# Reciprocal roots of the layer norms: a ScalarE seed with one Newton step in place of a bit guess with three

## The chip, the cores and the metric

The kernel runs on one core of a Trainium2 chip. The metric is the device time of one launch in microseconds; for a version with several runs it is their median. A core has five engines that work side by side, each through its own queue in order: TensorE (PE; its weight loads are listed apart as PEld), VectorE (DVE), ScalarE (ACT), GpSimd (POOL) and SyncE (SP). Engines wait for each other through semaphores. Transfers between memory and the core go through 16 DMA engines.

## The reference

The input is 32 images of 128 channels by 56 by 56. What is computed, cut to what matters:

```python
x = x + conv3x3(sign(groupnorm(x)), sign(w)) * Alpha      # layer 0
t = to_tokens(x)                                          # 32 x 3136 x 128
t = t + attention(_ln_t(t))       # q * sum(k * v), no softmax
t = t + top_2_of_8_experts(_ln_t(t))
x = from_tokens(t)

def _ln_t(v, eps=1e-5):
    m = jnp.mean(v, axis=-1, keepdims=True)
    s = jnp.var(v, axis=-1, keepdims=True)
    return (v - m) / jnp.sqrt(s + eps)
```

So each token needs two reciprocal roots of (variance + eps), one for each layer norm: the first scales the attention's inputs, the second the router's logits and the experts' inputs.

## The kernel before

**Tiling.** One image after another is worked on, in steps that overlap with those of the images before and after. Its 3136 tokens are 25 chunks of 128 (the last has 64), so that a number for each token of an image is a tile of 128 x 25 in float32. Chunks go in blocks of four (seven blocks), and the convolution in seven strips of eight rows.

**The stages of one image.** Group-norm sums on ScalarE (L579), a matmul for the group means (L592), signs on ScalarE (L599), the convolution (L642) and its addition on VectorE (L653), transposes to tokens (L667) with ScalarE's copies out of PSUM (L673), and the first statistics (L682). Then come the variance (`var_of`, L500 to L505) and the reciprocal root (`rstd_of`, L511 to L527). With it ScalarE scales the tokens (L735), TensorE makes their Gram matrix (L744), and a chain of small steps that alternate between TensorE and VectorE makes the attention's factor (L754 to L808). Projections (L863), their eviction with the root as the scale (L877), additions and the second statistics (L890, L893) follow, then the second variance and root. The router uses it: logits (L951 to L955), two largest experts (L938 to L962), their ratio as an exponential on ScalarE (L973), gates (L977 to L1012).

**Experts.** The first 8 to 12 chunks of an image go densely through all experts: gate rows are spread from memory (tile `bc`), VectorE multiplies (L1141), TensorE accumulates (L1159, in pool `ff`), VectorE adds (L1170). The other chunks of the first 28 images are sorted by pair of experts. GpSimd scatters their rows (L1365), and after each group of images (8, 8, 8 and 4) tiles of 128 rows are loaded, turned (L1669, L1675), multiplied by the two experts' weights (L1687), scaled by ScalarE (L1705, L1712), added (L1717, L1722), stored, gathered by GpSimd (L1444), turned back (L1459) and copied out (L1467).

**The order.** `plan_image` and `plan_group` enter each step with a due time, an engine, an assumed duration and the steps that it comes after (`at`). `in_order` is a list scheduler that takes these numbers and writes one order for all engines. A step whose work is given as a list of durations is split into links, with a lag of 0.12 us assumed between them, and the planner may put other work between two links. The order of each engine's queue is that order; the chip then runs each queue strictly in it. What the planner assumes therefore decides the order, not the time.

**The lines of the change.** `rstd1` and `rstd2` (steps due at s + 44 and s + 119, where s is the image's base time) call `rstd_of`. It has eleven VectorE instructions on 128 x 25: a shift of the variance's bits (L511), a subtraction from a constant (L518), which together give a first guess, and three Newton steps of three instructions each (L523, L525, L527), each needing the result of the one before. 32 images with two norms make 64 such roots. The three constants are filled at the start (L247 to L255). The convolution weights come through seven transfers issued from ScalarE's queue (L323 to L326), summed on VectorE (L350), and made into signs on ScalarE (L356). PSUM has a pool `ps` of five buffers, shared by most steps.

Of the kernel before, what the change touches and what calls it, by code (L numbers as in the profile page):

```python
# [46 lines left out]
I32 = mybir.dt.int32  # L47
U32 = mybir.dt.uint32
AF = mybir.ActivationFunctionType
ALU = mybir.AluOpType  # L50
# [4 lines left out]
C = 128  # L55
# [21 lines left out]
    mybir.EngineType.SP,  # L77
}
ON_POOL = 8
NEWTON = 3  # L80
IN_FLIGHT = 4
HELD, LOADS, LOAD_LANDS = 3, 4, 10.0

# [102 lines left out]
def conv_attn_moe_kernel(  # L186
# [19 lines left out]
    nc = tc.nc  # L206
    n_img, _, height, width = x.shape
    n_tok = height * width
    n_conv = height // ROWS
    n_ck = -(-n_tok // C)  # L210
# [24 lines left out]
    const = ctx.enter_context(tc.tile_pool(name="const", bufs=1))  # L235
# [11 lines left out]
    nc.vector.memset(ones, 1.0)  # L247
    ones_h = const.tile([C, C], BF16, name="ones_h")
    nc.vector.memset(ones_h, 1.0)
    one_i = const.tile([C, 1], I32, name="one_i")  # L250
    nc.vector.memset(one_i, 1)
    guess = const.tile([C, 1], I32, name="guess")
    nc.vector.memset(guess, 0x5F3759DF)
    m_one = const.tile([C, 2], F32, name="m_one")
    nc.vector.memset(m_one, -1.0)  # L255

# [61 lines left out]
    for j in range((K_REP + 1) // 2):  # L318
        flat = tok_all[j].rearrange("p c e -> p (c e)")
        z_sb += [flat[:, : TAPS * C], flat[:, TAPS * C : 2 * TAPS * C]]  # L320
    for k in range(2):
        load_x(0, nc.sync, k, 2)
    nc.scalar.dma_start(rv_bc, rv.to_broadcast([C, K_REP]))  # L323
# [144 lines left out]
    def at(due, key, engine, work, do, *args, after=(), take=(), free=(), delay=0.0, slack=0.0):  # L468


        if isinstance(work, float):
            steps[key] = Step(due, key, engine, work, do, args, after, take, free, delay, slack, 0.0)
            return
        running = []

        def go_on():
            if not running:
                running.append(do(*args))
            next(running[0], None)

        lag = LAG if isinstance(work, list) else 0.0
        for j, w in enumerate(work):
            last = j == len(work) - 1
            part = key if last else (*key, "part", j)
            steps[part] = Step(
                due, part, engine, w, go_on, (), [(*key, "part", j - 1)] if j else after,
                [] if j else take, free if last else [], delay if last else 0.0, slack, lag,
            )
# [6 lines left out]
    def var_of(stats, var, name):  # L495
# [8 lines left out]
        yield  # L504
        nc.vector.scalar_tensor_tensor(var, var, 1.0 / C, diff, ALU.mult, ALU.add)  # L505

    def rstd_of(var, dst, name):

        square = spool.tile([C, n_ck], F32, tag=f"square{name}", bufs=1, name="square")
        shape = [C, n_ck]  # L510
        nc.vector.tensor_tensor(  # L511
            square.bitcast(I32),
            var.bitcast(I32),
            one_i.to_broadcast(shape),
            ALU.logical_shift_right,
        )
        yield
        nc.vector.tensor_tensor(  # L518
            dst.bitcast(I32), guess.to_broadcast(shape), square.bitcast(I32), ALU.subtract
        )  # L520
        for _ in range(NEWTON):
            yield
            nc.vector.tensor_mul(square, dst, dst)  # L523
            yield
            nc.vector.scalar_tensor_tensor(square, square, -0.5, var, ALU.mult, ALU.mult)  # L525
            yield
            nc.vector.scalar_tensor_tensor(dst, square, 1.5, dst, ALU.add, ALU.mult)  # L527

    def sent_from(i, g):

# [13 lines left out]
    def plan_image(i: int):  # L544
        s = base(i)
        d = {"x": x_all[i % HELD], "tok": tok_all[i % HELD]}
# [59 lines left out]
        for k in range(n_load):  # L606
# [3 lines left out]
                after=[("load", i, k - 1) if k else ("load", i - 1, 1)]  # L610
# [4 lines left out]
        for j in range(GN_PARTS):  # L615
# [6 lines left out]
                after=[("gn_neg", i), ("conv", i - 1, min(j + 1, n_conv - 1))],  # L622
# [3 lines left out]
            after=[("gn_sum", i, j) for j in range(GN_PARTS)],  # L626
# [4 lines left out]
            after=[("gn_mean", i), ("gn_sign", i - 2, GN_PARTS - 1)], free=[("ps", ("gn_mean", i))],  # L631
# [53 lines left out]
        def var1():  # L685
            d["var1"] = spool.tile([C, n_ck], F32, tag="var1", name=f"var1_{i}")
            d["r1"] = spool.tile([C, n_ck], F32, tag="r1", name=f"r1_{i}")
            yield from var_of(st1, d["var1"], "1")

        def rstd1():  # L690
            yield from rstd_of(d["var1"], d["r1"], "1")

        for b in range(n_conv):
            at(
                s + 5.5 * b, ("conv", i, b), "PE", 1.75, conv, b,
                after=[("gn_sign", i, j) for j in range(min(b + 2, GN_PARTS))]
# [5 lines left out]
                after=[("conv", i, b)], free=[("ps", ("conv", i, b))],  # L702
            )
        for g in range(n_blk):
# [5 lines left out]
                after=[("conv_add", i, b), ("xt", i, g - 1)] + sent_from(i - HELD, g),  # L710
# [4 lines left out]
                after=[("xt", i, g)], free=[("ps", ("xt", i, g))],  # L715
# [3 lines left out]
                after=[("xt_out", i, g), ("var1", i - 2)],  # L719
# [3 lines left out]
            after=[("stats1", i, g) for g in range(n_blk)]  # L723
            + [("project_out", i - 2, 8), ("rstd1", i - 1)],
        )
        at(s + 44, ("rstd1", i), "DVE", [0.10] * (2 + 3 * NEWTON), rstd1, after=[("var1", i)])


        def scaled(g):
# [87 lines left out]
        for g in range(n_blk):  # L817
# [3 lines left out]
                after=[("rstd1", i), ("scaled", i, g - 1), ("scaled", i - 1, last_b)], take=["y"],  # L821
# [3 lines left out]
                after=[("scaled", i, g), ("gram", i, g - 1), ("kv_7", i - 1)],  # L825
# [90 lines left out]
        def var2():  # L916
            d["var2"] = spool.tile([C, n_ck], F32, tag="var2", name=f"var2_{i}")
            d["r2"] = spool.tile([C, n_ck], F32, tag="r2", name=f"r2_{i}")
            yield from var_of(st2, d["var2"], "2")

        def rstd2():
            yield from rstd_of(d["var2"], d["r2"], "2")

# [147 lines left out]
            after=[("project_add", i, j) for j in range(last_q + 1)]  # L1071
            + [("rstd2", i - 1), ("dense_gates", i - 2), ("row_scalars", i - 2)],
        )
        at(s + 119, ("rstd2", i), "DVE", [0.10] * (2 + 3 * NEWTON), rstd2, after=[("var2", i)])
        at(s + 125, ("route_1", i), "DVE", [0.28] * 3, route_1, after=[("rstd2", i)] + routed)
        at(s + 126, ("route_2", i), "DVE", [0.28] * 6, route_2, after=[("route_1", i)])
        at(s + 128, ("route_3", i), "DVE", [0.28] * 4 + [0.38], route_3, after=[("route_2", i)])
# [800 lines left out]
```

## Time and profile before

| | |
|---|---|
| median of 3 runs | 2172.5 us (2171.1 to 2178.69) |
| the profiled execution, in all | 2270.18 us |
| its span, first to last instruction | 2268.4 us |
| mean granted TensorE clock | 0.975 of full speed |
| ScalarE activation table loads | 1, 1283 ns (L579) |
| the five lines of `rstd_of`, VectorE busy | 11.5 + 11.4 + 34.7 + 35.1 + 34.6 us |

The profiled execution takes longer than the runs without a profile, so a saving that is read from it is carried over as a share. In the profile's tables, each group of instructions has one row: line, engine, operation, what it writes and reads, shape, count, then busy time in us, mean ns of one, and the idle time of the engine just before them with what ended it. A row of waits reads: engine and line that waited, what it waited for, us in total, times, the longest. A row of a stage reads: from and to in us, length, then busy us and count of each engine, TensorE's granted clock, the DMA engines' mean busy share and GB/s. Busy time on VectorE counts overlapping records once.

### The profile page before, as it was taken

The page shows a single profiled execution, that of the slowest core. Times are in us where ns is not written, and L with a number is a line of the kernel's source. Part 1 is how long each engine was busy: PE and PEld are TensorE (multiplying, and loading weights), DVE is VectorE, ACT ScalarE, POOL GpSimd, SP SyncE. Part 2 cuts the span into 40 slices and gives each one's busy share as a digit, 9 for nine tenths or more (in the row PEclk, how much of TensorE's full clock was granted, in tenths as well). Part 3 has the DMA queues.
Part 4 walks back from the last instruction along what each step waited for, and adds up shares of the span by engine and source line. Part 5 has one row for each costly group of instructions (what it writes and reads, how often), then busy time and mean ns, then how long its engine had stood idle before and what let it go on. Part 6 is the DMA issues. An engine that isn't in the chain of part 4 may idle for free.

```text
span 2268.4 us, 45320 instructions
## 1 busy us (share of the span) xinstructions
PE 2103.4 (93%) x12074; PEld 1449.1 (64%) x12074; DVE 1970.1 (87%) x6074; ACT 1531.2 (68%) x4917; POOL 1041.1 (46%) x1013
## 2 busy tenths in 40 slices
PE   5899999899999999789999999988999999999888
PEld 2666656557777776457676776655676666676544
DVE  4899999999989999688888889988898798789865
ACT  5667776668888887468777867655877776574311
POOL 3044443333433325466443644676654446233563
PEclk9989999999999999899999999999999999999999
DMA  4155544465665565377667766667767777878788
GB/s 166 30 175 177 167 153 141 138 184 184 203 186 165 176 181 168 110 219 252 194 202 220 226 198 202 215 214 240 225 195 232 217 203 247 249 214 270 222 278 273
DMA packets 324364, 448.58 MB, mean 198 GB/s; under 512 B 61832, under 2 KB 222128, under 8 KB 324112
## 3 DMA queue, kind: packets, MB, share of 16 engines
q1 hardware_dynamic: 294384, 382.80, 54.7%
q0 software_dynamic: 28144, 56.14, 8.2%
q10 hardware_dynamic: 1584, 6.75, 0.8%
q8 instruction: 102, 1.67, 0.3%
q14 instruction: 150, 1.23, 0.2%
HBM read 319.51 MB, written 126.00 MB: 196 GB/s over the span
## 4 chain that ended last, share of the span: by engine, by line
PE 42%; DVE 5%; DMA 3%; issue 2%; ACT 2%; another core or an unknown queue 1%; SPq 0%; POOL 0%; DVEq 0%; ACTq 0%; POOLq 0%
PE ff L1159 14%; PE to L1687 7%; PE cv L642 6%; PE q L863 3%; PE gram L744 3%; PE turn L1669 2%; PE back_ps L1459 2%; PE xt L667 2%; DVE gated L1141 1%; DMA back<-res,res_no 1%; PE l L1114 1%; DMA out_dram<-o 1%; PE ff L1153 1%; DMA bc<-gp 0%
## 5 line engine op out<-in xcount | busy, mean ns | idle before, releaser
L1365 POOL DMA_INDIRECT rows<-tok,row_no x428 | 524.3, 1225 | 570.5 <-ACT tok L1358 235.8
L1159 PE MATMUL ff<-gated,ew_d 128*128 128x512 f32 (+1 forms) x1536 | 711.5, 592 | 23.8 <-DVE gated L1141 19.8
L1444 POOL DMA_INDIRECT back<-res,res_no x428 | 485.4, 1134 | 464.1 <-PE back_ps L1459 264.1
L1141 DVE TENSOR_TENSOR gated<-tt,bc 128x1024 f32<-128x1024 f32 x384 | 450.7, 1180 | 92.2 <-PE ff L1159 29.9
L642 PE MATMUL cv<-xs,w_bin 128*128 128x440 bf16 (+3 forms) x2016 | 429.8, 362 | 18.5 <-ACT xs L599 10.0
L1159 PEld LDWEIGHTS ff<-gated,ew_d 128*128 128x128 f32 x1536 | 274.5, 193 | 258.6 <-issue 202.2
L1705 ACT ACTIVATE v<-to,t_in 128x128 f32<-128x128 f32 x528 | 255.3, 484 | 138.1 <-PE to L1687 74.6
L642 PEld LDWEIGHTS <-w_bin 128*128 128x128 bf16 x2016 | 200.1, 100 | 187.8 <-issue 38.3
L1687 PEld LDWEIGHTS to<-ew_s,turned 128*128 128x128 f32 x2112 | 260.8, 194 | 57.8 <-issue 32.4
L877 ACT ACTIVATE qs<-q,r 128x136 f32<-128x136 f32 (+1 forms) x800 | 247.6, 406 | 70.3 <-PE q L863 35.1
L1687 PE MATMUL to<-ew_s,turned 128*128 x2112 | 273.3, 279 | 18.2 <-ACT turned L1675 8.1
L735 ACT ACTIVATE y<-tok,r 128x128 f32<-128x128 f32 (+1 forms) x800 | 257.0, 428 | 24.3 <-PE gram L744 10.4
L863 PE MATMUL q<-move,x 128*128 128x144 f32 (+1 forms) x1600 | 239.9, 295 | 12.7 <-issue 3.7
L863 PEld LDWEIGHTS q<-move,x 128*128 128x128 f32 (+1 forms) x1600 | 213.6, 193 | 42.4 <-issue 21.1
L744 PEld LDWEIGHTS gram<-y 128*128 128x128 f32 (+1 forms) x1600 | 203.3, 192 | 53.9 <-issue 40.4
L744 PE MATMUL gram<-y 128*128 128x129 f32 (+1 forms) x1600 | 217.8, 281 | 12.9 <-issue 8.1
L682 DVE BATCH_NORM_STATS2 st<-tok 128x6 f32<-128x128 f32 (+1 forms) x800 | 185.4, 279 | 31.9 <-ACT tok L673 26.9
L1712 ACT ACTIVATE w<-to,t_in 128x128 f32<-128x128 f32 x528 | 208.6, 395 | 0.0
L893 DVE BATCH_NORM_STATS2 st<-tok 128x6 f32<-128x128 f32 (+1 forms) x800 | 198.1, 284 | 6.3
L673 ACT COPY tok<-xt 128x512 f32<-128x512 f32 (+1 forms) x224 | 121.2, 561 | 99.9 <-PE xt L667 71.6
L653 DVE SCALAR_TENSOR_TENSOR x<-cv,alpha_col,x 128x448 f32<-128x448 f32 x224 | 151.3, 676 | 40.1 <-PE cv L642 7.2
L890 DVE TENSOR_TENSOR tok<-tok,qs 128x408 f32<-128x408 f32 (+1 forms) x288 | 156.1, 542 | 29.4 <-ACT tok L882 24.1
(229 smaller groups left out, 2896.0 us busy)
## 6 DMA issues: line engine op xcount, KB each, us to landing
bc<-gp SPq DMA_DIRECT2D x368, 512.0 KB
x<-in_x_dram SPq DMA_DIRECT2D x116, 392.0 KB
t_in<-rows SPq DMA_DIRECT2D x528, 66.0 KB
res<-v SPq DMA_DIRECT2D x132, 256.0 KB
out_dram<-o SPq DMA_DIRECT2D x100, 256.0 KB
out_dram<-tt SPq DMA_DIRECT2D x92, 256.0 KB
rows<-zeros SPq DMA_DIRECT2D x116, 66.0 KB
rows<-tok,row_no POOLq DMA_INDIRECT x428
```

What stands on the lines that cost most here:

```text
L642: nc.tensor.matmul(cv[:, r0:r1, c0:c1], lhsT=w_bin[:, t, :], rhs=xs[:, b * ROWS + dy + r0 : b * ROWS + dy + r1, dx + c0 : dx + c1], start= ...
L735: nc.scalar.mul(y[:n, j, :C], d["tok"][:n, c, :C], d["r1"][:n, c : c + 1])
L744: nc.tensor.matmul(d["gram"], lhsT=y[:n, j, :C], rhs=y[:n, j, :], start=(c == 0), stop=(c == n_ck - 1),)
L863: nc.tensor.matmul(p[:n, k, :], lhsT=d["x"][:, c * C : c * C + n], rhs=move, start=True, stop=True,)
L877: nc.scalar.mul(qs[:n, k, :], p[:n, k, : C + N_EXP], d["r1"][:n, c : c + 1])
L1141: nc.vector.tensor_tensor(g[:, :, :n], d["tt", b][:, :n].unsqueeze(1).to_broadcast([C, 2, n]), d.pop(("bc", b, k))[:, :, :n], ALU.mult,)
L1159: nc.tensor.matmul(d["ff", b][:, :n], lhsT=ew_d[:, e * C : (e + 1) * C], rhs=g[:, j, :n], start=False, stop=(e == N_EXP - 1),)
L1365: dma = nc.gpsimd.indirect_dma_start(out=groups[group]["rows"], out_offset=bass.IndirectOffsetOnAxis(ap=d["row_no"][:n, c - n_dense : c - ...
L1444: dma = nc.gpsimd.indirect_dma_start(out=d["back", c][:n, :], out_offset=None, in_=groups[group]["res"][: quads_of(group) * WIDE, :], in_o ...
L1687: nc.tensor.matmul(p[:, k, j, :], lhsT=t[:, n * C : (n + 1) * C], rhs=ew_s[:, bass.ds(d["cols", q][j][n], C)], start=True, stop=True,)
L1705: nc.scalar.activation(d["v", q][:, n, :], p[:, k, 0, :], AF.Identity, bias=row[:, C + 2 : C + 3], scale=row[:, C : C + 1],)
L1712: nc.scalar.mul(d["w", q][:, n, :], p[:, k, 1, :], row[:, C + 1 : C + 2])
```

## The change

The two instructions of the bit guess and two of the three Newton steps go. A new helper, `seed_of`, has ScalarE write the logarithm of the variance and then, in place, the exponential of minus half of it. Two new steps, `seed1` and `seed2`, each with an assumed 0.45 us of ScalarE, stand between variance and root; the root has three VectorE links left. The two integer constants go, and at the start of the kernel the activation table set that has both functions is loaded ahead of the first transfers.

```diff
-NEWTON = 3
...
-    one_i = const.tile([C, 1], I32, name="one_i")
-    nc.vector.memset(one_i, 1)
-    guess = const.tile([C, 1], I32, name="guess")
-    nc.vector.memset(guess, 0x5F3759DF)
...
+    nc.scalar.preload_act_table_set("natural_log_exp_and_others")
     for k in range(2):
         load_x(0, nc.sync, k, 2)
     nc.scalar.dma_start(rv_bc, rv.to_broadcast([C, K_REP]))
...
+    def seed_of(var, dst):
+        nc.scalar.activation(dst, var, AF.Ln)
+        nc.scalar.activation(dst, dst, AF.Exp, scale=-0.5)
+
     def rstd_of(var, dst, name):
 
         square = spool.tile([C, n_ck], F32, tag=f"square{name}", bufs=1, name="square")
-        shape = [C, n_ck]
-        nc.vector.tensor_tensor(
-            square.bitcast(I32),
-            var.bitcast(I32),
-            one_i.to_broadcast(shape),
-            ALU.logical_shift_right,
-        )
+        nc.vector.tensor_mul(square, dst, dst)
         yield
-        nc.vector.tensor_tensor(
-            dst.bitcast(I32), guess.to_broadcast(shape), square.bitcast(I32), ALU.subtract
-        )
-        for _ in range(NEWTON):
-            yield
-            nc.vector.tensor_mul(square, dst, dst)
-            yield
-            nc.vector.scalar_tensor_tensor(square, square, -0.5, var, ALU.mult, ALU.mult)
-            yield
-            nc.vector.scalar_tensor_tensor(dst, square, 1.5, dst, ALU.add, ALU.mult)
+        nc.vector.scalar_tensor_tensor(square, square, -0.5, var, ALU.mult, ALU.mult)
+        yield
+        nc.vector.scalar_tensor_tensor(dst, square, 1.5, dst, ALU.add, ALU.mult)
...
+        def seed1():
+            seed_of(d["var1"], d["r1"])
+
...
-        at(s + 44, ("rstd1", i), "DVE", [0.10] * (2 + 3 * NEWTON), rstd1, after=[("var1", i)])
+        at(s + 43, ("seed1", i), "ACT", 0.45, seed1, after=[("var1", i)])
+        at(s + 44, ("rstd1", i), "DVE", [0.10] * 3, rstd1, after=[("seed1", i)])
...
+        def seed2():
+            seed_of(d["var2"], d["r2"])
...
-        at(s + 119, ("rstd2", i), "DVE", [0.10] * (2 + 3 * NEWTON), rstd2, after=[("var2", i)])
+        at(s + 118, ("seed2", i), "ACT", 0.45, seed2, after=[("var2", i)])
+        at(s + 119, ("rstd2", i), "DVE", [0.10] * 3, rstd2, after=[("seed2", i)])
```

## The prediction

> **What bounds the kernel now.** I read the page's first two parts, then the table of busy time by stage, because an average over a kernel whose mixture of work changes says little.
>
> ```profile
> PE 2103.4 (93%) x12074; PEld 1449.1 (64%) x12074; DVE 1970.1 (87%) x6074; ACT 1531.2 (68%) x4917; POOL 1041.1 (46%) x1013
> ```
>
> TensorE is busy for 93% of the span, VectorE for 87%. Only 165 us of the span have no matmul, and that is all that any change away from TensorE can win. By stage (length, then busy us of each engine):
>
> ```profile
> core 0: us, PE busy (x) PEld busy (x) DVE busy (x) ACT busy (x) POOL busy (x), PEclk, DMA share, GB/s
> 120.00:540.00 420.00, 392.64 (x2204) 257.30 (x2203) 407.87 (x1428) 289.34 (x969) 179.95 (x164) 0.98 0.50 161
> 540.00:900.00 360.00, 353.04 (x2277) 260.40 (x2277) 337.96 (x1065) 304.50 (x995) 136.62 (x110) 1.00 0.60 181
> 900.00:1500.00 600.00, 561.73 (x3296) 392.91 (x3295) 525.36 (x1644) 433.60 (x1398) 319.70 (x272) 0.97 0.68 209
> 1500.00:1920.00 420.00, 386.19 (x2296) 275.81 (x2295) 349.98 (x1057) 292.60 (x925) 236.35 (x206) 0.97 0.73 217
> 1920.00:2100.00 180.00, 179.88 (x978) 122.51 (x977) 155.41 (x368) 103.16 (x319) 58.98 (x52) 1.00 0.81 244
> 2100.00:2268.40 168.40, 143.17 (x520) 78.41 (x519) 113.21 (x214) 32.23 (x92) 85.71 (x74) 0.93 0.79 258
> ```
>
> From 120 to 540 us VectorE sets the pace: 12.1 us idle of 420, while TensorE idles 27.4. From 540 to 900 TensorE does (7.0 idle of 360). From 900 to 1920 neither is full (TensorE idle 72.1, VectorE 144.7 of 1020), so chains between engines end the waits there. From 1920 to 2100 TensorE never stops; after that the tail waits for transfers. The first 120 us, with 33.2 us of TensorE idle, are the start.
>
> The lines that the change touches, and two waits:
>
> ```profile
> L525 DVE SCALAR_TENSOR_TENSOR square<-square,var 128x25 f32<-128x25 f32 x192 | 35.1, 183 | 3.3
> L523 DVE TENSOR_TENSOR square<-r 128x25 f32<-128x25 f32 x192 | 34.7, 181 | 2.9 <-DVE r L527 0.2
> L511 DVE TENSOR_TENSOR square<-var,one_i 128x25 int32<-128x25 int32 x64 | 11.5, 180 | 0.7
> L973 ACT ACTIVATE ratio<-ratio 128x25 f32<-128x25 f32 x32 | 7.8, 243 | 46.1 <-DVE ratio L970 27.1 <-DVE best L944 5.6 <-DVE res_no L1439 5.3
> ```
>
> ```profile
> PE ff L1159 <- DVE gated L1141: 19.8, 20, 2.6
> ACT ratio L973 <- DVE ratio L970: 27.1, 14, 4.3
> ```
>
> The second line of the pair is the nearest relative of what is added: an exponential of a 128x25 tile on ScalarE, between two VectorE steps.
>
> The timeline of VectorE at one root (start, duration) shows how much the links really occupy:
>
> ```profile
> 377.77 0.17 DVE L511 TENSOR_TENSOR square<-var,one_i 128x25 int32<-128x25 int32 x1
> 377.86 0.29 DVE L893 BATCH_NORM_STATS2 st<-tok 128x6 f32<-128x128 f32 x1
> 378.06 0.17 DVE L518 TENSOR_TENSOR r<-guess,square 128x25 int32<-128x25 int32 x1
> 378.14 1.22 DVE L1141 TENSOR_TENSOR gated<-tt,bc 128x1024 f32<-128x1024 f32 x1
> 379.28 0.18 DVE L523 TENSOR_TENSOR square<-r 128x25 f32<-128x25 f32 x1
> 379.37 0.58 DVE L890 TENSOR_TENSOR tok<-tok,qs 128x408 f32<-128x408 f32 x1
> ```
>
> A link is recorded as 0.17 us, but other work starts 0.09 us after it. Where nothing can be put between (at 336.9 us of the same timeline) links follow each other every 0.22 us. From start to next start, the links between 60 and 540 us take 0.144 us on average; later about 0.15 to 0.19.
>
> [...] The trace of before shows one load, 1.283 us (L579, at 8.15 us); no switch is in it. The changed kernel's instruction order holds one load too, the preload, so I count no switch. [...] the trace has a median of 226 and a mean of 243 for L973, and I use 0.23.
>
> **Part by part.** The sum is made against the profiled execution: span 2268.4, 2270.2 in all. That is 4.5% above the median of 2172.5, so I carry a share, not microseconds, over.
>
> Removed: 64 roots (32 images, two each), with 8 of 11 links gone: shift, subtraction and two Newton steps. 512 x 0.144 = 74 us of VectorE issue time; by recorded durations 512 x 0.18 = 92. Per root 8 x 0.144 = 1.15 us. Two constant fills at the start (0.06 us each) go as well: nothing waits for them, zero.
>
> Added on ScalarE: 128 activations x 0.243 = 31 us. Its idle time is 737 us, so as volume that is covered, least well from 540 to 900, where it is busy 304.5 of 360. The two are dependent, so one seed takes about 0.46 us.
>
> Added waits: logarithm for variance, Newton step for seed. The exponential of L973 starts 0.03 to 0.04 us after its input is written when ScalarE is free, and VectorE follows a ScalarE result in 0.03 at best; the free round trip is 0.04 + 0.46 + 0.03 = 0.53 us. In the changed order, VectorE has other work between variance and Newton step in 62 of 64 roots, most often two to five instructions, some 1.7 us by this trace's durations; in the VectorE-bound stage the second root's cover is mostly one 128x512 addition, 0.6 us. So a free ScalarE costs VectorE nearly nothing. A late one (L973 started up to 2.4 us late between 540 and 900) costs up to 2 us, behind which all of VectorE's queue stands, the gating products for TensorE first. Bounds per root: 0 and 2 us; I take 0.1. On the other side, the logarithm at the head of ScalarE's queue holds back what is queued behind it, evictions of matmul results above all, as L973 does: 46.1 us idle in 32 times, 1.44 each. TensorE has five PSUM buffers in hand against that. In the waits, TensorE stands for ScalarE 36.5 us between 120 and 1920; I let that grow by a tenth, 4 us (bounds 0 and 32, half a us for each root).
>
> What is late next, by stage. From 120 to 540, 16 roots free 16 x 1.15 = 18.4 us of a full VectorE; TensorE's floor, at the 1.9% idle that it reaches in the next stage, is 392.6 / 0.981 = 400, or 20 less. TensorE's waits put down to VectorE there are 10.7 us, to ScalarE 11.4, part of them VectorE's delay passed on. I take 12. From 540 to 900 TensorE is full: of 3.7 us of waits for VectorE I take 1.5. From 900 to 1500 the waits for VectorE are 12.5 us, but VectorE had 75 us of idle time and was late for other reasons: a third, 4. From 1500 to 1920, 10.8 us: a quarter, 3. After 1920: 0.5. From 60 to 120 one image runs nearly alone and the chain itself counts: eight links of 0.2 less a round trip of 0.53 is 1.1 us; 1.5 for both roots, not all on the path. Sum of gains 22.5.
>
> Moved: the table load goes from 8.15 us, where it kept ScalarE from sums that aren't late (the last weights arrive at 22.5 us), to the front of ScalarE's stream, ahead of seven weight transfers. If it holds their issue, they start 1.3 us later [...] on the path to the first convolution; if not, zero. I take 0.5. And the planner, which gets other work and dependences, reorders: a comparison of the two orders moves about a sixth of TensorE's matmuls, 253 of SyncE's 2721 entries and 27 of GpSimd's 1018, transfers among them. The added steps issue no transfer. Bounds -10 and +10 us, from the pieces of 1 to 3 us that TensorE waits at such places; I take zero.
>
> Costs: 16 x 0.1 = 1.6, 4 and 0.5, about 6. Net -16.5 us: 2270.2 becomes 2253.7, a factor 0.9927; x 2172.5 = 2157 us.
>
> **Rivals.** (a) Relief on the covered side: TensorE's peak was the limit all along and the waits for VectorE only change their name. For it: TensorE at 98 to 100% in two stages, and an unprofiled run with 98 us less, in which there may be little idle time to win. Gains and costs both about 6: 2166 to 2176, say 2171. Against it: the stage at 120 to 540.
> (b) The relief is passed on: all of TensorE's waits for VectorE after 60 us (some 50 us) and part of those for ScalarE close, 35 to 45 us less: 2172.5 x (1 - 40/2270) = 2134. Against it: VectorE had idle time after 900.
> (c) Slower: the logarithm at the head of ScalarE's queue. ScalarE stands for the variance as it stands for L970, 64 x 1.44 = 92 us, evictions come late, PSUM buffers run out and TensorE loses half a us for each root, 32 us, over the 16.5 + 4 that remain without it. That is +11.5 profiled: 2184. It cancels the gain from 0.32 us per root. For it: ScalarE is already 85% busy from 540 to 900. Against it: L973 waits that way 32 times, and of TensorE's waits only one, of 0.2 us, names it.
> That the change does not do what it says (a table switch for each seed, 128 x 1.3 us) is excluded by the single load in the order.
>
> **How the numbers follow.** Forecast 0.46 (2147 to 2166), (a) 0.29, (b) 0.12, (c) 0.13. The range reaches to 2133 and 2183: half of (b) and most of (c) lie outside, some 17 in 100. A measurement of this kernel tells 0.5% (11 us) from no change. Faster by more takes all of (b) and 0.41 of the forecast: 0.54 with a little of (a); slower is (c), 0.13; within is the rest, 0.33.
>
> **What would show it.** Right: VectorE's busy time near 1970 - 92 = 1880, ScalarE's near 1562; from 120 to 540 an image every 48 to 49 us instead of 50 (spacing of the group-mean matmuls, L592), TensorE there 95 to 96% busy; hardly any VectorE wait named for the exponential. Wrong: VectorE idle before the first Newton link of over 0.3 us per root; TensorE's waits for ScalarE up by over 15 us; idle time merely moved to the stages after 900; more than one table load; the first convolution later than 26 us.

## The result, and the profile after

The change makes the kernel a little slower: 2189.1 us (9 runs, 2183.6 to 2195.8) against 2176.7 us (9 runs, 2171.1 to 2182.6), a ratio of 1.0058, 95% interval 1.0040 to 1.0076. The forecast was 2157 us.

The profiled execution of the changed kernel took 2189.1 us, its median. That of before, from which the prediction was worked out, took 94 us more than its median. Profiled once more (the run again_before below), the kernel before took 2168.4 us with a span of 2166.7, so it is not profiling that made the first one long. The two executions agree up to image 10, whose group-mean matmul comes at 470 and at 469 us; image 16's comes at 848 and 837, and most of the rest is lost later: image 31's comes at 2003 and 1909. In the last series of runs below, on another chip, the kernel before had a median of 2262.6 us as well, for a reason that is not known, so ratios are taken within a series. What follows compares the changed kernel with again_before.

Busy time by stage of the changed kernel (from and to, length, then busy us of each engine, TensorE's granted clock, DMA share, GB/s):

```profile
120.00:540.00 420.00, 388.63 (x2174) 255.94 (x2172) 389.40 (x1281) 291.66 (x982) 171.45 (x162) 0.96 0.47 152
540.00:900.00 360.00, 356.57 (x2323) 265.09 (x2322) 333.12 (x993) 315.95 (x1047) 128.47 (x112) 1.00 0.62 191
900.00:1500.00 600.00, 585.42 (x3499) 411.46 (x3500) 550.02 (x1643) 462.02 (x1502) 347.71 (x299) 0.99 0.74 223
1500.00:1920.00 420.00, 409.38 (x2489) 295.68 (x2487) 358.15 (x954) 314.27 (x1004) 225.29 (x194) 1.00 0.81 239
```

and of the kernel before in its second profile:

```profile
120.00:540.00 420.00, 393.48 (x2231) 258.02 (x2229) 412.08 (x1442) 295.29 (x990) 185.26 (x167) 0.99 0.51 166
540.00:900.00 360.00, 353.94 (x2299) 263.27 (x2300) 344.89 (x1098) 312.14 (x1020) 138.90 (x113) 1.00 0.61 188
900.00:1500.00 600.00, 589.46 (x3542) 415.76 (x3542) 565.52 (x1789) 455.56 (x1467) 352.99 (x302) 0.99 0.73 224
1500.00:1920.00 420.00, 412.33 (x2518) 299.01 (x2517) 374.44 (x1043) 316.66 (x994) 218.95 (x192) 1.00 0.82 242
```

VectorE was relieved: from 120 to 540 us it is busy 389 us instead of 412. TensorE, which should have moved into the room, is busy less too, 389 instead of 393, and at a lower granted clock, 0.96 instead of 0.99. The difference in clock is an estimated 420 x 0.03, roughly 13 us of full-speed TensorE, more than the 5 us by which its idle time grew. From 540 to 1920 us the stages hardly differ.

The group-mean matmul of image 4 comes at 163 us (before: 169), image 5 at 211 (212), image 6 at 268 (264), image 7 at 320 (311), image 10 at 477 (469), image 16 at 845 (837), image 31 at 1919 (1909). So the start is faster by 6 us, 15 us are lost between images 4 and 7, and 8 to 10 us of delay stay until image 31. The two spans differ by 21 us. The other half comes after image 31's group means, from which the changed kernel takes 268 us to its end and the kernel before 258. The experiments below look at the early part; the end was not followed up.

The lines that replace the eleven links:

```profile
L504 ACT ACTIVATE r<-var 128x25 f32<-128x25 f32 x64 | 16.4, 257 | 10.4 <-DVE var L501 10.1
L505 ACT ACTIVATE r<-r 128x25 f32<-128x25 f32 x64 | 14.4, 226 | 2.0
L510 DVE TENSOR_TENSOR square<-r 128x25 f32<-128x25 f32 x64 | 11.4, 178 | 6.7 <-ACT r L505 6.7
L512 DVE SCALAR_TENSOR_TENSOR square<-square,var 128x25 f32<-128x25 f32 x64 | 11.6, 181 | 0.8
L514 DVE SCALAR_TENSOR_TENSOR r<-square,r 128x25 f32<-128x25 f32 x64 | 11.5, 179 | 0.9
```

The seeds take 30.8 us of ScalarE, as foreseen, and both waits that they bring are small in total: ScalarE 10.1 us for the variance, VectorE 6.7 us for the seed. What grew is another wait, which names no root. Waits of TensorE from 160 to 540 us, in the changed kernel and then before:

```profile
PE ff L1154 <- DVE gated L1136: 23.3, 8, 5.3
```

```profile
PE ff L1159 <- DVE gated L1141: 1.4, 5, 0.4
```

TensorE stands at the first expert matmul until VectorE has made the gating product. Five of these waits, one in each of five images in a row (from 225 to 431 us), take 3.8 to 5.3 us; the other three together take 2.6. TensorE's rows of the changed kernel at such a place (start, duration, idle before it):

```profile
375.26 0.39 PE L1148 MATMUL ff<-gt,eb_w 72*128 72x512 bf16 x1
379.48 5.40 PE L1154 MATMUL ff<-gated,ew_d 128*128 128x512 f32 x8 [3.82 <-DVE gated L1136]
```

the kernel before at the same step:

```profile
371.12 0.39 PE L1153 MATMUL ff<-gt,eb_w 72*128 72x512 bf16 x1
371.86 3.70 PE L1159 MATMUL ff<-gated,ew_d 128*128 128x512 f32 x8 [0.35 <-DVE gated L1141]
```

and VectorE of the changed kernel during the wait:

```profile
375.20 0.68 DVE L884 BATCH_NORM_STATS2 st<-tok 128x6 f32<-128x128 f32 x3
375.80 1.04 DVE L669 BATCH_NORM_STATS2 st<-tok 128x6 f32<-128x128 f32 x5
376.87 0.20 DVE L496 TENSOR_TENSOR diff<-st 128x25 f32<-128x25 f32 x1
...
377.93 0.17 DVE L501 SCALAR_TENSOR_TENSOR var<-var,diff 128x25 f32<-128x25 f32 x1
378.01 0.29 DVE L884 BATCH_NORM_STATS2 st<-tok 128x6 f32<-128x128 f32 x1
378.22 2.34 DVE L1136 TENSOR_TENSOR gated<-tt,bc 128x1024 f32<-128x1024 f32 x2
```

VectorE is not waiting here: it works through its queue, in which statistics and variance stand ahead of the product that TensorE needs. That is a matter of the planner's order. Over the whole stage from 120 to 540 us VectorE nevertheless idles 30.6 us, against 7.9 before, 16.9 of it for TensorE's results in `kv_ps` and `ff`: the two engines wait for each other in turn, and the room that the change made on VectorE becomes idle time there. As other waits of TensorE got shorter, its idle time in the stage grew by 5 us only (31.4 against 26.5), not by the 22 of this one wait.

### The profile page after: what moved, and what is told of

The parts are those of the page before. It is cut to its first block, busy times and chain, and to the rows that moved or that the text cites. A ratio compares the mean times of both kernels' runs of the same rounds, so it can differ in the third digit from the quotient of the medians.

```text
span 2187.4 us, 44888 instructions
## 1 busy us (share of the span) xinstructions
PE 2072.8 (95%) x12074; PEld 1438.0 (66%) x12074; DVE 1907.9 (87%) x5560; ACT 1553.1 (71%) x5045; POOL 1029.2 (47%) x1013
## 3 DMA queue, kind: packets, MB, share of 16 engines
q8 instruction: 102, 1.67, 0.3%
## 4 chain that ended last, share of the span: by engine, by line
PE 69%; DVE 16%; DMA 9%; issue 3%; ACT 2%; SPq 1%; POOL 1%; DVEq 0%; POOLq 0%; ACTq 0%
PE ff L1154 24%; PE cv L629 13%; PE to L1682 9%; PE gram L735 7%; PE q L854 5%; DMA bc<-gp 3%; PE xt L654 3%; DVE gated L1136 2%; PE turn L1664 2%; DVE st L884 2%; DMA back<-res,res_no 2%; DVE st L669 2%; DVE tok L881 2%; PE back_ps L1454 2%; DVE tok L806 1%
## 5 line engine op out<-in xcount | busy, mean ns | idle before, releaser
L1360 POOL DMA_INDIRECT rows<-tok,row_no x428 | 497.6, 1163 | 570.9 <-ACT tok L1353 287.3
L1154 PE MATMUL ff<-gated,ew_d 128*128 128x512 f32 (+1 forms) x1536 | 721.0, 600 | 37.7 <-DVE gated L1136 37.3
L1439 POOL DMA_INDIRECT back<-res,res_no x428 | 502.1, 1173 | 392.9 <-PE back_ps L1454 204.0
L1154 PEld LDWEIGHTS ff<-gated,ew_d 128*128 128x128 f32 x1536 | 280.2, 196 | 277.7 <-issue 205.4
L629 PE MATMUL cv<-xs,w_bin 128*128 128x440 bf16 (+3 forms) x2016 | 419.0, 355 | 7.3 <-ACT xs L586 7.1
L669 DVE BATCH_NORM_STATS2 st<-tok 128x6 f32<-128x128 f32 (+1 forms) x800 | 182.3, 276 | 19.6 <-ACT tok L660 19.1
L884 DVE BATCH_NORM_STATS2 st<-tok 128x6 f32<-128x128 f32 (+1 forms) x800 | 190.1, 283 | 7.6
L881 DVE TENSOR_TENSOR tok<-tok,qs 128x408 f32<-128x408 f32 (+1 forms) x288 | 155.3, 539 | 31.9 <-ACT tok L873 31.4
```

The source lines that it names most:

```text
L629: nc.tensor.matmul(cv[:, r0:r1, c0:c1], lhsT=w_bin[:, t, :], rhs=xs[:, b * ROWS + dy + r0 : b * ROWS + dy + r1, dx + c0 : dx + c1], start= ...
L884: nc.vector.bn_stats(st2[:n, c, :], d["tok"][:n, c, :C])
L1154: nc.tensor.matmul(d["ff", b][:, :n], lhsT=ew_d[:, e * C : (e + 1) * C], rhs=g[:, j, :n], start=False, stop=(e == N_EXP - 1),)
L1360: dma = nc.gpsimd.indirect_dma_start(out=groups[group]["rows"], out_offset=bass.IndirectOffsetOnAxis(ap=d["row_no"][:n, c - n_dense : c - ...
L1439: dma = nc.gpsimd.indirect_dma_start(out=d["back", c][:n, :], out_offset=None, in_=groups[group]["res"][: quads_of(group) * WIDE, :], in_o ...
```

## The experiments

**Theory O**: the new order costs, not the new instructions. **Theory S**: the hop to ScalarE costs. **Theory P**: TensorE hides everything. The first series separates work from order.

*again_before*: no edit.

> The kernel before, unchanged, profiled once more, because its first profiled execution (2270 us) was 94 us longer than the median of its runs (2176.7), while that of the changed kernel was not longer than its median (2189). Both theories expect 2171 to 2183 us, and a span near 2175. If the first profile only had a long middle and end, VectorE's idle time from 120 to 540 us is again near 12 us, and the idle time of TensorE there near 25.

Measured: 2168.4 us, a little under what was expected. The idle time of VectorE from 120 to 540 us was 7.9 us and TensorE's 26.5. From 900 to 1920 TensorE idled 18.2 us, not 72.1 as in the first profile.

*seed_old_order*: the whole change, planned as before.

```diff
+    nc.scalar.preload_act_table_set("natural_log_exp_and_others")
...
+        nc.scalar.activation(dst, var, AF.Ln)
+        nc.scalar.activation(dst, dst, AF.Exp, scale=-0.5)
+        for _ in range(2 + 3 * (NEWTON - 1)):
+            yield
+        nc.vector.tensor_mul(square, dst, dst)
...
```

> The whole change with every other instruction in the order of before: the planner still plans eleven links of VectorE, the first of them issues both ScalarE activations, eight issue nothing, the last three are the Newton step. If the planner's new order is what costs (theory O), this is faster than before: 0.990 to 0.997 of it, 2155 to 2170 us. If the hop to ScalarE and its queue cost (theory S), it is slower than before by about as much as the change: 1.004 to 1.010. If TensorE hides all (theory P), 0.998 to 1.002.

Measured: 0.9964 (0.9950 to 0.9978) of before, 2165.8 us. In the old order the change gains.

*old_math_new_order*: the changed kernel's plan with the old arithmetic.

```diff
     def seed_of(var, dst):
-        nc.scalar.activation(dst, var, AF.Ln)
-        nc.scalar.activation(dst, dst, AF.Exp, scale=-0.5)
+        pass
...
```

> The order of the changed kernel with the arithmetic of before: no activation is issued, and the eleven VectorE instructions stand at the three places of the Newton step (five, three, three). Theory O expects this to be slower than the changed kernel by what the removed links are worth: 1.008 to 1.016 of before. Theory S expects it near before or a little over it, since no engine is crossed: 0.998 to 1.004. Theory P expects it near the changed kernel, 1.004 to 1.008.

Measured: 1.0218 (1.0203 to 1.0233), 2220.0 us, more than any theory gave. The eleven links stand back to back at three places here, which is unkind to them (where nothing stood between two links, in the first profile of before at 336.9 us, they started 0.22 us apart; on average from 60 to 540 us 0.144), so this run does not price the order by itself. It does show the wait without any seed: TensorE's waits for the gating product are 27.3 us from 160 to 540, much as in the changed kernel.

*fewer_links_old_order*: two Newton steps left out, order of before.

```diff
-        for _ in range(NEWTON):
+        for k in range(NEWTON):
+            if k < 2:
+                for _ in range(3):
+                    yield
+                continue
             yield
```

> Order and arithmetic of before with two of the three Newton steps left out (384 VectorE instructions less, so the roots are only good to about a thousandth); nothing is added on ScalarE. It prices the relief of VectorE by itself. By the prediction's sum it should be worth three quarters of 22 us: 0.991 to 0.994 of before. Theory O expects 0.990 to 0.996, theory S the same, theory P 0.998 to 1.002.

Measured: 0.9930 (0.9917 to 0.9943). The relief of VectorE by six links of eleven is worth 15 us; theory P falls, and S cannot explain the change, which gains in the old order. So O: 1.0058 / 0.9964 = 1.0094, about 20 us, is what the new order costs with the same instructions. But seed_old_order, with two links fewer still, keeps only half of the relief. Both are followed up.

The second series alters the order alone, and takes the seed apart.

*seed_plan_050*: one number of the plan.

```diff
-        at(s + 43, ("seed1", i), "ACT", 0.45, seed1, after=[("var1", i)])
+        at(s + 43, ("seed1", i), "ACT", 0.50, seed1, after=[("var1", i)])
...
-        at(s + 118, ("seed2", i), "ACT", 0.45, seed2, after=[("var2", i)])
+        at(s + 118, ("seed2", i), "ACT", 0.50, seed2, after=[("var2", i)])
```

> The changed kernel with one number of the planner altered: the seed is assumed to take 0.50 us of ScalarE instead of 0.45. The instructions are the same, only their order differs. The planner's own clock then has image 10's group means at 459.9 us instead of 471.8, and its end at 2176.4 instead of 2185.2. Theory O (the planner's order, not the seed, made the change slow, and which order comes out is chance): 0.993 to 0.999 of before, 2157 to 2170 us, and no waits of 4 us at the first expert matmuls of images 3 to 8. Theory S (the seed itself costs): as the changed kernel, 1.004 to 1.008.

Measured: 0.9997 (0.9983 to 1.0011), 2172.0 us; the same instructions as the change, 0.6% less time, a little short of what was expected. From 160 to 540 us TensorE waits for gating products:

```profile
PE ff L1154 <- DVE gated L1136: 4.9, 6, 1.7
```

instead of 23.3 us, and image 10's group means come at 461 us instead of 477. So the seed as such does not make the kernel slower than before.

*before_plan_011*: the kernel before, one number of the plan.

```diff
-        at(s + 44, ("rstd1", i), "DVE", [0.10] * (2 + 3 * NEWTON), rstd1, after=[("var1", i)])
+        at(s + 44, ("rstd1", i), "DVE", [0.11] * (2 + 3 * NEWTON), rstd1, after=[("var1", i)])
... (and the same for rstd2)
```

> The kernel before with one number of the planner altered: each link of a root is assumed to take 0.11 us instead of 0.10. Instructions are the same; the planner's own end goes from 2181.7 to 2189.3 us and image 10's group means from 462.8 to 470.0. If the order is as sensitive as theory O says, this is slower than before without any change of work: 1.003 to 1.007. If the planner's order is not what counts, 0.998 to 1.002.

Measured: 1.0030 (1.0021 to 1.0039), the lower edge of the band. No instruction differs from before; TensorE's waits for gating products are 15.1 us instead of 1.4.

*old_plan_first_8*: eleven planned links for images 0 to 7, the change's plan after.

```diff
+        if i < 8:
+            at(s + 44, ("rstd1", i), "DVE", [0.10] * 11, rstd1, after=[("var1", i)])
+        else:
+            at(s + 43, ("seed1", i), "ACT", 0.45, seed1, after=[("var1", i)])
+            at(s + 44, ("rstd1", i), "DVE", [0.10] * 3, rstd1, after=[("seed1", i)])
... (and the same for rstd2; rstd_of issues the seed itself for these images)
```

> The changed kernel with the planner told of eleven links and no seed for images 0 to 7 (the activations go out with the first link), and of the seed as in the change from image 8 on. If the loss of the change is made in the stage from 160 to 330 us, as the positions of the group-mean matmuls say, this keeps the relief and loses nothing: 0.992 to 0.997 of before, 2155 to 2166 us. If the order after image 8 costs too, it stays over 1.000.

Measured: 0.9977 (0.9967 to 0.9987), a little over the expected band. Planning the early images as before removes the loss, so most of it hangs on their plan: image 10's group means come at 467 us instead of 477. From image 12's group means on, TensorE's order is the change's in all but 154 of 8999 matmuls, and there the end keeps its length: 265 us from image 31's group means, as in the changed kernel (268).

*unread_seed_old_order* and, in a later series, *unread_const_old_order*: fewer_links_old_order with both activations added, read by nobody, once of the variance and once of a constant.

```diff
+        idle = spool.tile([C, n_ck], F32, tag=f"idle{name}", bufs=1, name="idle")
+        nc.scalar.activation(idle, var, AF.Ln)
+        nc.scalar.activation(idle, idle, AF.Exp, scale=-0.5)
...
```

In unread_const_old_order the first activation reads `ones[:, :n_ck]` instead of `var`.

> Order of before, two of three Newton steps left out as in fewer_links_old_order, and both activations issued at each root with the variance as input, into a tile that nothing reads. The roots come from the bit guess, good to about a thousandth. ScalarE thus carries the seed's load and its wait for the variance, and VectorE never waits for ScalarE. fewer_links_old_order took 0.9930, seed_old_order 0.9964. If the difference is VectorE's wait for the seed, this takes 0.9925 to 0.9940; if it is ScalarE's load and its wait for the variance, 0.9955 to 0.9970.

> As unread_seed_old_order (two Newton steps left out, the roots good to about a thousandth, both activations issued and read by nothing), but with a constant tile as their input: ScalarE carries the load at the same place of its queue and waits for nothing. Wait theory: 0.9925 to 0.9945. Load theory: 0.9965 to 0.9980.

Measured: 0.9973 (0.9961 to 0.9984) with the variance, 0.9936 (0.9922 to 0.9950) with the constant. 128 activations as such cost nothing that can be measured (0.9936 against 0.9930). ScalarE's wait for the variance costs 0.37%, 8 us, with VectorE never waiting for ScalarE's result. From 120 to 540 us, TensorE's waits for the convolution's signs are longer with the variance than with the constant:

```profile
PE cv L650 <- ACT xs L607: 14.0, 8, 2.8
```

```profile
PE cv L650 <- ACT xs L607: 11.1, 5, 2.8
```

These 2.9 us are all by which TensorE's idle time differs there (23.2 and 20.3 us). The granted clock is 0.97 and 0.99, an estimated 420 x 0.02, roughly 8 us of full-speed time; the two digits are coarse, and part of it falls into the waits. Image 10's group means come at 466 and 459 us, so most of the 8 us are lost by then. How it happens, ScalarE's row of seed_old_order shows at one place:

```profile
319.66 0.23 ACT L511 ACTIVATE r<-var 128x25 f32<-128x25 f32 x1 [1.09 <-DVE var L506]
319.92 0.23 ACT L512 ACTIVATE r<-r 128x25 f32<-128x25 f32 x1
320.05 0.39 ACT L1350 ACTIVATE tok<-tok,a 128x128 f32<-128x128 f32 x1
320.34 1.22 ACT L591 ACTIVATE xs<-x,neg_gm 128x448 bf16<-128x448 f32 x2
```

The signs (L591) that the convolution needs stand behind the logarithm. TensorE waits 2.83 us for the first strip of them, much as in the kernel before (2.85), and then waits again for the second, and the clock falls:

```profile
318.63 1.24 PE L634 MATMUL cv<-xs,w_bin 128*128 128x448 bf16 x6 [2.83 <-ACT xs L591]
321.05 1.28 PE L634 MATMUL cv<-xs,w_bin 128*128 128x440 bf16 x3 [1.18 <-ACT xs L591]
322.12 0.63 PE L1145 MATMUL ff<-gt,eb_w 72*128 72x512 bf16 x1
322.55 5.71 PE L1151 MATMUL ff<-gated,ew_d 128*128 128x512 f32 x8
```

fewer_links_old_order at the same step, with one wait:

```profile
317.05 2.61 PE L646 MATMUL cv<-xs,w_bin 128*128 128x448 bf16 x9 [2.84 <-ACT xs L603]
319.45 0.63 PE L1157 MATMUL ff<-gt,eb_w 72*128 72x512 bf16 x1
319.88 4.32 PE L1163 MATMUL ff<-gated,ew_d 128*128 128x512 f32 x8
```

Windows of four microseconds around it, in seed_old_order:

```profile
316.00:320.00 4.00, 1.24 (x6) 0.58 (x6) 3.93 (x18) 2.88 (x12) 2.98 (x4) 1.00 0.91 325
320.00:324.00 4.00, 2.95 (x6) 1.41 (x6) 3.94 (x8) 4.00 (x12) 2.60 (x4) 0.50 0.50 156
324.00:328.00 4.00, 4.00 (x7) 1.49 (x6) 2.88 (x9) 4.00 (x14) 1.92 (x3) 0.65 0.61 197
```

and in fewer_links_old_order:

```profile
316.00:320.00 4.00, 2.95 (x11) 1.52 (x11) 3.97 (x14) 4.00 (x14) 2.79 (x4) 0.74 0.60 208
320.00:324.00 4.00, 4.00 (x9) 1.60 (x8) 3.93 (x16) 3.52 (x12) 2.87 (x4) 0.84 0.82 242
324.00:328.00 4.00, 4.00 (x19) 2.25 (x18) 3.95 (x9) 4.00 (x16) 2.70 (x3) 1.00 0.68 210
```

The granted clock (third number from the right) is 0.50 and 0.65 in the two windows after the first wait, and 0.74 and 0.84 with the single wait. The matmuls of these windows count as busy (the eight expert matmuls 5.71 us here and 4.32 there): part of what a wait costs shows as busy time.

*seed_late_old_order*: the activations at the fifth link.

```diff
-        nc.scalar.activation(dst, var, AF.Ln)
-        nc.scalar.activation(dst, dst, AF.Exp, scale=-0.5)
-        for _ in range(2 + 3 * (NEWTON - 1)):
+        for j in range(2 + 3 * (NEWTON - 1)):
+            if j == 4:
+                nc.scalar.activation(dst, var, AF.Ln)
+                nc.scalar.activation(dst, dst, AF.Exp, scale=-0.5)
             yield
...
```

(The lines are compared with seed_old_order.)

> As seed_old_order (the whole change, every other instruction in the order of before), but the two activations are issued at the fifth of the eleven planned links instead of the first, so that ScalarE meets the logarithm when the variance is long written and the convolution's signs are not held behind it. If ScalarE's wait for the variance at the head of its queue is what took half of the relief (1.09 us at 318 us, then 1.18 us of TensorE waiting for signs and a granted clock of 0.5 for four us), this takes 0.9920 to 0.9945 of before, 2156 to 2162 us. If it is the mere time of the 128 activations, it stays at 0.9955 to 0.9975. If VectorE now waits for the seed, over 0.998.

Measured: 0.9949 (0.9933 to 0.9965), 2163.3 us, between the two bands. ScalarE's waits for the variance are gone from the early stage; VectorE waits more for the seed instead, 7.6 us from 120 to 540 after 1.9. It has the lowest ratio to before of all versions that compute the roots in full, but its interval overlaps with seed_old_order's, so the gain over that one is not shown.

*fewer_links_replanned*: two Newton steps left out and the planner told.

```diff
-NEWTON = 3
+NEWTON = 1
```

> Two of three Newton steps left out (roots good to about a thousandth) and the planner told of it: five links. The planner's own end is 2173.5 us, against 2181.7 for before, with image 10's group means at 462.3 against 462.8. In the order of before this work took 0.9930. If any new order is as likely to be worse as better, 0.990 to 0.999; if the planner's own clock ranks the orders on the chip, 0.992 to 0.996.

Measured: 0.9955 (0.9936 to 0.9974). No seed is involved, and the new order again seems to lose part of what the same work gains in the old one (0.9930, to 0.9943; the intervals just overlap): from 120 to 540 us TensorE waits 19.2 us for gating products. The result lies in both bands that were named, so it doesn't separate them.

*gates_earlier*: the changed kernel with the first two gating products of images 2 to 7 moved ahead by fourteen VectorE steps.

```diff
-        for step in in_order(steps):
+        order = in_order(steps)
+        for i in range(2, 8):
+            for k in range(2):
...
+                while to > floor + 1 and passed < 14:
+                    to -= 1
+                    passed += order[to].engine == "DVE"
+                order.insert(to, gate)
+        for step in order:
...
```

> The changed kernel with twelve VectorE instructions moved and nothing else: the first two gating products of images 2 to 7 stand fourteen VectorE steps earlier in its queue, ahead of the statistics and the variance instead of behind them. If TensorE's six waits of 1.7 to 5.3 us at the first expert matmuls (23.3 us in 160 to 540 us) and the lower granted clock after each are the loss, about 3 us for each of the six come back, part of it given away by later statistics: 0.996 to 1.001 of before, 2164 to 2176 us, and the waits shrink to a third. If those waits only stand in for some other lateness of the order (the gate rows' transfers, for one, which VectorE would then wait for), it stays at 1.004 to 1.007.

Measured: 1.0079 (1.0061 to 1.0098), no gain at all, and over the higher of the two bands. From 160 to 480 us:

```profile
PE gram L735 <- ACT y L726: 20.5, 5, 4.2
ACT r L504 <- DVE var L501: 11.8, 6, 2.5
PE ff L1154 <- DVE gated L1136: 6.4, 6, 1.9
```

The wait for gating fell from 22.5 us to 6.4, and another took its place: variance and seed are now late, and TensorE stands about 4 us in each of five images at the Gram matrix that needs the scaled tokens. So the place of the gating product is where the loss shows; moving it alone does not undo the loss. In this order VectorE comes late with one or the other. TensorE's granted clock in this stretch is 0.95, where the changed kernel has 0.96. Of the changed kernel's six waits named above, five were followed by a lower clock (0.50 to 0.65 in the lowest window of four microseconds); after the shortest, of 1.67 us, it was 1.00.

The last series asks whether a planned seed is slow as such. *seed_plan_030*, *seed_plan_060*, *seed_plan_070*: the edit of seed_plan_050 with 0.30, 0.60 and 0.70.

> The changed kernel, the seed's assumed duration 0.30 us; same instructions. The planner's own end is 2177.6 us, image 10's group means at 465.1 (before: 2181.7 and 462.8; the change: 2185.2 and 471.8). If order is chance and the planner's clock at image 10 ranks it, between seed_plan_050 and the change: 0.999 to 1.004. If a planned seed is always slow, 1.004 to 1.008.

> The changed kernel, assumed duration 0.60 us; same instructions. The planner's own end is 2179.7 us, image 10's group means at 472.3. If the clock at image 10 ranks the orders, as slow as the change: 1.003 to 1.008. If the planner's end ranks them, 0.998 to 1.002.

> The changed kernel, assumed duration 0.70 us; same instructions. The planner's own end is 2190.3 us, image 10's group means at 474.3, the slowest of the plans tried. By either clock the slowest on the chip: 1.005 to 1.010. If order is chance that the planner's clock does not see, anywhere from 0.996 to 1.010.

Measured: 1.0020 (0.9994 to 1.0045), 1.0043 (1.0019 to 1.0067) and 1.0101 (1.0070 to 1.0132), each against the kernel before in this series: the first two inside the band that the planner's clock at image 10 suggested, the third just above its own. Seven orders beside the planner's own clock, which is a sum of assumed durations and no measurement:

| kernel | planner: image 10's group means | planner: end | ratio to before |
|---|---|---|---|
| change, seed 0.50 | 459.9 | 2176.4 | 0.9997 |
| before | 462.8 | 2181.7 | 1 |
| change, seed 0.30 | 465.1 | 2177.6 | 1.0020 |
| before, links 0.11 | 470.0 | 2189.3 | 1.0030 |
| the change, seed 0.45 | 471.8 | 2185.2 | 1.0058 |
| change, seed 0.60 | 472.3 | 2179.7 | 1.0043 |
| change, seed 0.70 | 474.3 | 2190.3 | 1.0101 |

The five plans of the change, with the same instructions, spread over 1% by an assumed duration alone: from 0.9997 to 1.0058 in the two earlier series, from 1.0020 to 1.0101 in the last. There is no steady trend in the number that was turned. The planner's clock at image 10 puts all seven in the measured sequence but for one neighbouring pair; its end does so less well. As several neighbours have intervals that overlap, this is a hint and not a proven rule.

## Why the prediction was wrong

**The planner's reordering, taken as zero with bounds of -10 and +10 us.** This is the step that failed. It measured 0.94%, 20 us: 1.0058 for the change against 0.9964 for the same instructions in the old order, twice the bound. The bound came from single waits of 1 to 3 us. In the early images one wait of 3.8 to 5.3 us comes back in five images in a row. From 120 to 540 us TensorE idles 31.4 us, against 22.0 in seed_old_order, at nearly the same clock (0.96 and 0.97), and image 10's group means come 12 us later (477 against 466). The images from 10 to 31 win back 6 us, and the stretch from image 31 to the end is 12 us longer (268 against 256). That the order could cost this much was foreseeable in kind: the prediction counted a sixth of TensorE's matmuls as moved and then priced that at nothing.

**The relief of VectorE, 22.5 us of gains.** Right in mechanism and about right in size: six links of eleven gave 15 us in the old order. That VectorE sets the pace from 120 to 540 us held too: in the profile of fewer_links_old_order, image 10's group means come 10 us earlier than in again_before (459 against 469), where three quarters of the 12 taken would be 9. The terms for 900 to 1920 us, 7 of the 22.5, rest on 72 us of TensorE idle time that belonged to the one long execution; the second profile has 18. In the same two profiles nothing more is gained there: image 31's group means come 11 us earlier, and the end 10.

**ScalarE, 4 us, and VectorE's wait, 1.6.** The mechanism was the right one, and is rival (c)'s: the logarithm at the head of the queue. In the old order it was mis-sized: 8 us (0.9973 against 0.9936) against 4 taken; rival (c) had 32. From 120 to 540 us it acted not through PSUM evictions but through the signs of the convolution (14.0 us of waits against 11.1) and the granted clock (0.97 against 0.99). In the changed kernel it has little part in the early loss: ScalarE waits for the variance 1.3 us from 120 to 540, against 8.3 in seed_old_order. VectorE's wait is small, as said: 6.7 us in all in the changed kernel, 0.1 per root.

**The rivals.** (a) fell with fewer_links_old_order, and (b), 35 to 45 us, was not reached by it: 15 us for six of eight links. (c), the only one on the right side, named 2184 us, near the measured 2189, by luck: it put 32 us on the head of ScalarE's queue, which measured 8, and nothing on the order, which measured 20. That the load of tables might hold up the transfers is off: the last group of weight transfers was issued at 1.75 us in both kernels, and the load (1.28 us, from 0.82 us) ran beside them. It is the only table load in the changed kernel's profile: none came between the logarithms and the exponentials of the 64 seeds.

**The signs that were named.** VectorE busy fell by 57 us (1965.4 to 1907.9), not 92, because removed links had overlapped with their neighbours (0.17 us recorded, the next start after 0.09, at 377.77 us of the first profile): the 74 of issue time is nearer. ScalarE is at 1553, against 1562 foreseen. From image 4 to image 10 an image takes 52 us, where 50 was to become 48 to 49, and TensorE is busy for 92.5% of 120 to 540 us, not 95 to 96. TensorE's waits for ScalarE did not grow (18.9 us before, 13.1 after), its waits for VectorE did (67.9 to 76.9).

**What stays open.** Why the scheduler falls into the slower pattern with shorter work is not settled. gates_earlier shows that the gating products' place alone isn't it; which placement would undo the pattern wasn't found. The 10 us that the changed kernel's profile loses after image 31's group means were not examined either.

## What to carry to other kernels

Where a list scheduler writes the order, a change has two effects, the work and the new order; build it once in the old order (the removed links as empty steps) to price them apart, and turn one assumed duration by a tenth to see how much order alone is worth before believing a change of under 1%. What the short steps on another engine cost here was what stood behind them in that queue while they waited: 128 activations cost nothing that can be measured with their input at hand (0.9936 against 0.9930 without them) and 8 us when they waited (0.9973). Issuing them later took that wait away and gave another to VectorE; a net gain was not shown. Compare a profile's own time with the median before reading idle time from it.

## What the runs showed of the hardware

In these places a short wait of TensorE (2.84 us, and 2.83 with 1.18 us) was paid for a second time, in granted clock (0.74 and 0.84, and 0.50 and 0.65). The windows of four microseconds above give an estimate: one minus the clock, times 4 us, is the full-speed time lost. After the single wait of 2.84 us that is 4 x (0.26 + 0.16), about 1.7 us; after the waits of 2.83 and 1.18 us it is 4 x (0.50 + 0.35), 3.4 us. How much of it the next matmuls feel differs. In unread_const_old_order, after a single wait of 2.85 us, the loss falls into one window:

```profile
316.00:320.00 4.00, 3.26 (x10) 1.36 (x10) 3.97 (x13) 3.97 (x14) 3.02 (x4) 0.57 0.52 191
320.00:324.00 4.00, 4.00 (x13) 1.77 (x12) 3.93 (x16) 3.87 (x13) 2.90 (x3) 1.00 0.86 275
```

It is 4 x 0.43, again 1.7 us, and the eight expert matmuls that began at 320.16 us took 3.60 us, where they took 4.32 and 5.71 in the two kernels above. After 3.82 us of waiting the changed kernel's took 5.40, with a clock of 0.57 from 380 to 384 us and 1.00 in the windows on either side. At its four other waits of 3.8 to 5.3 us for gating products (the matmuls begin at 224.58, 276.75, 328.42 and 430.59 us) the eight took 6.49, 6.00, 5.40 and 5.40 us, and the lowest window had a clock of 0.50, 0.50, 0.65 and 0.62. After waits of 1.67 and 0.76 us (172.31 and 501.03 us) they took 3.70 and 3.99 us, with 1.00 in the windows around them.
